# Seven products in place of eight for the left half of the first slice, and for one quarter product of each other slice

## The chip, the cores and the metric

One NeuronCore of a Trainium2 chip runs the whole program. The metric is the device time of one execution in microseconds (us), here the median of three. Every number of the page and the trace comes from one profiled execution; times in the trace count from the start of its span. TensorE multiplies matrices (PE, with PEld for its weight loads), VectorE (DVE) and ScalarE (ACT) do elementwise work, GpSimd (POOL) and SyncE (SP) mostly start transfers. A matmul here has float32 operands, and the trace shows each as two records.

## The reference

Four layers over `x` (8 batches, 2048 nodes, 64 features), each ending in a residual sum and a layernorm. All of them multiply `adj` (2048 x 2048) with the nodes, twice in most layers:

```python
# layer 0: three terms, the node's own weights made from its embedding
As = [I, A, 2 A A - I]
x_g = einsum('knm,bmc->bnkc', stack(As), x)
x = layernorm(x + einsum('bnki,nkio->bno', x_g, einsum('nd,dkio->nkio', emb, weight)) + emb @ bias)
# layer 1: z = relu((A z) w_i), twice.   x = layernorm(x + z)
# layer 2: x = layernorm(x + x w_self + (A x) w_neigh + b)
# layer 3: [x, A x, 2 A A x - x] twice, times weight, + b, then the same
```

The change concerns the first of these products, `A x` of layer 0, and some weights that stand beside it.

## The kernel before

Nodes stand on 128 partitions in 16 tiles, and the 8 batches make 4 pairs of 128 columns: `xy[:, t, slot, pair]`. A product `A x` is 2048 x 2048 by 2048 x 512.

Later products (`product`, from L211) are made of seven quarter products in place of eight, and each quarter product again of seven; the names A11, A12, A22 and S1 to S4 are the seven left operands (quarters of `adj` or sums of quarters). Each needs eight blocks of `adj` or of sums of its blocks, read from DRAM: plain blocks from `in_blocks`, and sums from `comb`, 1 MB a load.

Nothing has made those sums at the start. So the first product runs in the *slice stage*, over four slices `ns` of four row tiles each (tiles `ns`, `ns + 4`, ...). A slice of `adj` is loaded as four chunks of 512 columns (`slice_chunk`, L152, 1 MB each) into a ring of four buffers `a`. While TensorE multiplies a slice, `prepare` (L638) has VectorE form its share of all sums of `adj`, and GpSimd's queue stores them in `comb` (`keep`, L655). `outer` makes S1 to S4 of two half chunks each (tag "T", three buffers; each a pair of sums of 128x1024, so 1 MB), `inner` makes the four inner sums of a quarter (tag "C", four buffers, four sums of 128x512). A chunk's buffer is free when TensorE and all of these sums have read it. The last sum to read chunks 0 and 1 is S3's outer sum.

- *Slice 0* is plain (`plain_slice`, L783): 64 matmuls of 512 columns, in the order of chunks 2, 3, 0, 1 (`AHEAD`), for four pairs into four PSUM banks. Meanwhile VectorE makes the sums, and `sums_of_x` (L749) the four sums T1 to T4 of quarters of x.
- *Slices 1 to 3* (`fast_slice`, L807) use seven quarter products, of 16 matmuls with 256 columns each (`mul`, L825): A12 (`p2`), A22 with T4 (`pd`), A11 (`pa`), S1 with T1, S2 with T2, S4, S3 with T3. The first two read chunks 2 and 3 alone, `pa` chunks 0 and 1. Results are joined in `hT` (`done`, L839), whose copy is stored as `t1T` by SyncE's queue (`keep_t1`, L770) and transposed back into `xy` (`back`, L779, by `to_nodes` L453) between later matmuls.

Loads of chunks, of weights, the `t1T` stores and later `a`, `xT`, `tT` loads all go through SyncE's queue, in an order that the tile scheduler made; GpSimd's queue holds the `comb` stores, `e_sb`, and later its own sums. `wn`, layer 0's weights, is loaded on SyncE's queue at L592 and summed (differences and centring, `sum_wn` L604) in slice 2. It's first used by `feature0` (L954, matmuls at L970) after the first two of the next product's seven quarter products.

Where an instruction is wrapped in `keep_in_program_order`, the scheduler leaves it in the order of the program among those of its engine that are wrapped too. In slice 0 the sums are not wrapped, in slices 1 to 3 they are.

Of the kernel before, what the change touches and what calls it, by code (L numbers as in the profile page):

```python
# [16 lines left out]
P = 128  # L17
# [3 lines left out]


A11, A12, A22, S1, S2, S3, S4 = range(7)

# [77 lines left out]
def kernel(  # L104
# [470 lines left out]


    if True:
        l0 = first.enter_context(tc.tile_pool(name="l0", bufs=1))

        wn = l0.tile([P, 3, D, F], F32, tag="wn", name="wn")  # L580

        def center(w, half=slice(0, P), pin=lambda inst: inst):
            shape = list(w.shape)
            m = small.tile([P, shape[1]], F32, tag="wm", name="wm")[half]
# [3 lines left out]
            ))  # L588

        def load_weights():  # L590
            for k in range(2):
                nc.sync.dma_start(wn[k * F : (k + 1) * F], w_l0.rearrange("n i d o -> i n d o"))  # L592
            nc.gpsimd.memset(wd, 0.0)
            w3 = sums.tile([P, 5, F], F32, tag="t", name="w3", bufs=5)
            for k in range(2):
                half = slice(k * F, (k + 1) * F)
                for i, src in ((W1A, w_l1[0]), (W1B, w_l1[1]), (W2N, w_neigh), (W2S, w_self)):
                    nc.sync.dma_start(wd[half, i, half], src)
                nc.scalar.dma_start(w3[half], w_l3.rearrange("(k i) o -> i k o", i=F))
            nc.sync.dma_start(b2, b_l2.to_broadcast([P, F]))  # L600
            nc.sync.dma_start(b3, b_l3.to_broadcast([P, F]))
            return w3

        def sum_wn():  # L604
            pin = tc.keep_in_program_order
            pin(nc.vector.tensor_tensor(wn[:, 0], wn[:, 0], wn[:, 2], ALU.subtract))
            pin(nc.vector.tensor_scalar(wn[:, 2], wn[:, 2], 2.0, None, ALU.mult))
            center(wn.rearrange("p n d o -> p (n d) o"), pin=pin)

        def sum_weights(w3):  # L610
            pin = tc.keep_in_program_order
# [26 lines left out]
        def prepare(ns, ch, outers):  # L638

            ch = [c.rearrange("p m i n -> p i m n") for c in ch]  # L640

            def add(out, a, b, op=ALU.add):
                inst = nc.vector.tensor_tensor(out, a, b, op)
                if ns:

                    tc.keep_in_program_order(inst)

            def kept(tag, shape, bufs):
                s = sums.tile([P, *shape, GW], F32, tag=tag, name="s" + ("i" if tag == "C" else "o"), bufs=bufs)
                n = "ab"[: len(shape)]  # L650
                return s, s.rearrange(f"p {' '.join(n)} (m n) -> p {' '.join(n)} m n", m=TG)

            def keep(q, s0, src):
                dst = comb[q][s0 : s0 + src.shape[1]].rearrange("s p (n c) -> p s n c", n=TG)
                nc.gpsimd.dma_start(dst[:, :, ns], src)  # L655

            def inner(q, q00, q01, q10, q11):
                flat, s = kept("C", (4,), 4)
                add(s[:, 0], q10, q11)
                add(s[:, 1], s[:, 0], q00, ALU.subtract)  # L660
                add(s[:, 2], q00, q10, ALU.subtract)
                add(s[:, 3], q01, s[:, 1], ALU.subtract)
                keep(q, 4, flat)

            def raw(I, J):
                return [ch[2 * J + b][:, 2 * I + a] for a in range(2) for b in range(2)]

            def outer(a, b, op):

                flat, s = kept("T", (2, 2), 3)  # L670
                for c in range(2):
                    add(s[:, :, c], a(c), b(c), op)
                return flat

            def rq(I, J):
                return lambda c: ch[2 * J + c][:, 2 * I : 2 * I + 2]

            def sq(s):
                return lambda c: s[:, :, c].rearrange("p a (m n) -> p a m n", m=TG)

            def put(q, s):
                flat = s.rearrange("p a b c -> p (a b) c")
                keep(q, 0, flat[:, :2])
                keep(q, 3, flat[:, 3:])
                inner(q, *(flat[:, k].rearrange("p (m n) -> p m n", m=TG) for k in range(4)))


            inner(A12, *raw(0, 1))
            inner(A22, *raw(1, 1))
            outers[S1] = s1 = outer(rq(1, 0), rq(1, 1), ALU.add)  # L690
            outers[S2] = s2 = outer(sq(s1), rq(0, 0), ALU.subtract)
            outers[S4] = s4 = outer(rq(0, 1), sq(s2), ALU.subtract)
            yield
            put(S1, s1)
            yield
            put(S2, s2)
            inner(A11, *raw(0, 0))
            yield
            outers[S3] = s3 = outer(rq(0, 0), rq(1, 0), ALU.subtract)
            yield  # L700
            put(S3, s3)
            put(S4, s4)
            yield

        with tc.tile_pool(name="p_n", bufs=4, space=PSUM) as p_n, tc.tile_pool(
# [30 lines left out]
            def xq(h, c):  # L736

                v = xy[:, h * NT // 2 : (h + 1) * NT // 2, 0, c * 4 * F : (c + 1) * 4 * F]
                return v.rearrange("p (t h) c -> p t h c", h=2)
# [6 lines left out]
                xy[:, 2:NT:TG, 1, :].rearrange("p t (h c) -> p t h c", h=2),  # L746
            ]

            def sums_of_x():  # L749
                sub = ALU.subtract  # L750
                nc.vector.tensor_tensor(T[0], xq(0, 1), xq(0, 0), sub)
                nc.vector.tensor_tensor(T[1], xq(1, 1), T[0], sub)
                nc.vector.tensor_tensor(T[2], xq(1, 1), xq(0, 1), sub)
                nc.vector.tensor_tensor(T[3], xq(1, 0), T[1], sub)

            def join_bias(h, c):
                v = xq(h, c).rearrange("p t h (b f) -> p (t h) b f", f=F)
# [18 lines left out]
            def new_h():  # L776
                return sums.tile([P, GW], F32, tag="t", name="hT", bufs=5)

            def back(ns, p, hT):  # L779
                to_nodes(1, p_tn, slice(ns, NT, TG), p, hT)  # L780
                yield

            def plain_slice(ns, ch):  # L783

                ps = [bank() for p in range(NP)]
                for n, j in enumerate(AHEAD):
                    steps = [(p, m) for p in range(NP) for m in range(TG)]
                    if n == 0:

                        steps = [(p, m) for m in range(TG) for p in range(NP)]  # L790
                    for k, (p, m) in enumerate(steps):
                        mm = nc.tensor.matmul(  # L792
                            ps[p],
                            xcol(0, TG * j + m, p),
                            ch[j][:, m],
                            start=(n == 0 and m == 0),
                            stop=(n == NG - 1 and m == TG - 1),
                            skip_group_check=True,
                        )
                        if n == k == 0:  # L800
                            tc.keep_in_program_order(mm)
                hT = [new_h() for p in range(NP)]
                for p in range(NP):
                    nc.scalar.copy(hT[p], ps[p])
                return hT

            def fast_slice(ns, ch, held):  # L807


                outers = {}  # L810
# [41 lines left out]
                    return u  # L852

                next(parts)
                p2 = mul(bank(), raw(0, 1), x_of(1, 0))
                pd = mul(bank(), raw(1, 1), t_of(4))
                load_chunks(ns + 1, 2, 3)
                for job in held:
                    pump.add(back(*job))
# [1 line left out]
                pa = mul(bank(), raw(0, 0), x_of(0, 0))  # L861
                p1 = sums.tile([P, GW], F32, tag="p1", name="p1")
                nc.scalar.copy(p1, pa)
                q3 = plus("u3", pd, p1)
                done(0, p2, p1)
                if ns == TG - 1:
                    join_bias(0, 1)
# [3 lines left out]
                load_chunks(ns + 1, 0, 1)  # L871
                if ns == 1:
                    sum_weights(w3)
                elif ns == 2:
                    sum_wn()
                else:
                    join_bias(0, 0)
                pb_ = mul(bank(), summed(S2), t_of(2))
                u2 = plus("u2", pb_, p1)
# [13 lines left out]
            for ns in range(TG):  # L893
                ch = [chunks.pop((ns, j)) for j in range(NG)]
                if ns == 0:
                    for n, _ in enumerate(prepare(ns, ch, {})):
                        if n == 1:
                            sums_of_x()
                    hT = plain_slice(ns, ch)
                    w3 = load_weights()  # L900
                    load_chunks(1, *AHEAD)
                    pump.add(biases())
                else:
                    hT = fast_slice(ns, ch, held)
                for p in range(NP):
                    keep_t1(ns, p, hT[p])

                held = []
                for p in range(NP):
                    if ns == TG - 2:  # L910
                        held.append((ns, p, hT[p]))
                    else:
                        pump.add(back(ns, p, hT[p]))
# [20 lines left out]
        if True:  # L934
            p_y = first.enter_context(tc.tile_pool(name="p_y", bufs=3, space=PSUM))
            l0y = first.enter_context(tc.tile_pool(name="l0y", bufs=1))
            e_sb = l0y.tile([P, NT, D], F32, tag="e_sb", name="e_sb")
            nc.gpsimd.dma_start(e_sb, emb)


            order = [
# [51 lines left out]


            RUNS = {S2: NP, S3: NP}
            product(1, then(feature0, 0, gap=4, pool_sq=True), rate=4, runs=RUNS)


    late = p_z = None
# [127 lines left out]
```

## Time and profile before

| | us |
|---|---|
| three runs, median (lowest, highest) | 1670.58 (1670.14, 1670.74) |
| the profiled execution | 1670.91 |
| its span | 1669.1 |
| TensorE busy | 1660.6 |
| VectorE busy | 945.8 |
| slice 0's matmuls | 5.68 to 61.04 |
| slices 1 to 3, up to the first matmul of the next product | 61.04 to 216.15 |

The page gives busy time and instructions of each engine, then the chain of work that ended last, followed back from the last instruction. Groups and pieces read "line engine operation out<-in". A busy TensorE is a pipelined one: the records of one matmul overlap with the next, so what a matmul costs is the distance between starts.

### The profile page before, as it was taken

How to read it: one execution, taken by the hardware profiler on the slowest of the kernel's cores; microseconds unless marked ns; L12 is line 12 of the kernel's file. 1: busy time of each engine (PE TensorE's matmuls, PEld its weight loads, DVE VectorE, ACT ScalarE, POOL GpSimd, SP SyncE). 2: the span in 40 equal slices, each digit the busy share in tenths (PEclk: the TensorE clock that was granted, in tenths of full speed). 3: DMA queues.
4: the chain of work that ended last, by engine and by line, in shares of the span. 5: the costliest groups of instructions: out<-in, count | busy, mean ns of one | idle time of the engine just before them, and what ended most of it. 6: DMA issues, size and time to landing. Idle time of an engine off the chain costs nothing.

```text
span 1669.1 us, 20686 instructions
## 1 busy us (share of the span) xinstructions
PE 1660.6 (99%) x8182; PEld 1046.5 (63%) x8182; DVE 945.8 (57%) x1695; ACT 265.3 (16%) x766; POOL 246.0 (15%) x332
## 2 busy tenths in 40 slices
PE   9999999999999999999999999999999999999998
PEld 4688854444444444444454455589998455579998
DVE  6497884556456456654434365873568344443657
ACT  0100000142143044430010011220001011100001
POOL 1121200254155056650000000000000000000000
PEclk9999999999999999999999999999999999999999
DMA  9898898504603700019877877667888866678884
GB/s 352 331 373 310 302 334 307 189 27 147 227 26 108 271 26 26 26 51 369 286 264 272 308 263 253 229 225 260 297 297 295 306 212 232 229 267 292 316 308 171
DMA packets 82431, 391.52 MB, mean 235 GB/s; under 512 B 8896, under 2 KB 25536, under 8 KB 42784
## 3 DMA queue, kind: packets, MB, share of 16 engines
q1 hardware_dynamic: 69520, 346.78, 58.8%
q0 software_dynamic: 11248, 42.08, 6.6%
q10 hardware_dynamic: 1568, 1.35, 0.3%
q8 instruction: 65, 1.06, 0.3%
q14 instruction: 30, 0.25, 0.0%
HBM read 339.85 MB, written 50.33 MB: 234 GB/s over the span
## 4 chain that ended last, share of the span: by engine, by line
PE 98%; DMA 1%; DVE 0%; ACT 0%; issue 0%; ACTq 0%; DVEq 0%
PE y L970 20%; PE mmb L272 17%; PE mma L272 12%; PE mmc L272 12%; PE mmb L265 9%; PE ps_n L829 8%; PE mma L265 6%; PE mmc L265 6%; PE ps_n L792 3%; PE z L1022 3%; PE z L1051 2%; DMA a<-in_slices 1%; PE pt L1013 1%; DMA xy<-in_x 0%; PE pt_n L457 0%; PE mmd L265 0%
## 5 line engine op out<-in xcount | busy, mean ns | idle before, releaser
L272 PE MATMUL mmb<-a,t 128*128 128x512 f32 x648 | 292.0, 593 | 0.0
L980 DVE SCALAR_TENSOR_TENSOR xy<-y,e_sb,xy 128x128 f32<-128x128 f32 x512 | 179.6, 351 | 141.2 <-PE y L970 125.3
L272 PEld LDWEIGHTS mmb<-a,t 128*128 128x128 f32 x648 | 121.5, 190 | 145.3 <-issue 143.5
L989 POOL TENSOR_TENSOR s<-s 128x512 f32<-128x512 f32 (+2 forms) x192 | 157.1, 818 | 333.4 <-ACT s L984 323.2
L984 ACT ACTIVATE s<-y,e_sb 128x128 f32<-128x128 f32 x512 | 139.0, 382 | 231.8 <-PE y L970 231.8
L223 DVE TENSOR_TENSOR u<-mmb,p 128x512 f32<-128x512 f32 x84 | 57.8, 689 | 181.8 <-PE mmb L272 126.0
L265 PE MATMUL mmb<-t,a 128*128 128x128 f32 x1344 | 156.9, 275 | 0.0
L265 PEld LDWEIGHTS mmb<-t,a 128*128 128x128 f32 x1344 | 153.4, 192 | 0.0
L970 PE MATMUL y<-wn,xT 64*128 64x512 f32 x512 | 131.5, 590 | 0.0
L970 PE MATMUL y<-wn,tT 64*128 64x512 f32 x512 | 131.2, 589 | 0.0
L970 PE MATMUL y<-wn,C 64*128 64x512 f32 x512 | 131.2, 589 | 0.0
L272 PE MATMUL mma<-a,T 128*128 128x512 f32 x256 | 115.5, 594 | 0.0
L272 PE MATMUL mmc<-a,t 128*128 128x512 f32 x216 | 97.3, 592 | 0.0
L287 ACT COPY p<-mma 128x512 f32<-128x512 f32 x42 | 24.6, 586 | 404.4 <-PE mma L272 262.9
L970 PEld LDWEIGHTS y<-wn,xT 64*128 64x128 f32 x512 | 49.3, 187 | 61.2 <-issue 60.7
L970 PEld LDWEIGHTS y<-wn,tT 64*128 64x128 f32 x512 | 49.6, 187 | 60.3 <-issue 60.3
L970 PEld LDWEIGHTS y<-wn,C 64*128 64x128 f32 x512 | 49.6, 187 | 60.3 <-issue 60.3
L272 PE MATMUL mma<-a,xy 128*128 128x512 f32 x192 | 86.7, 593 | 0.0
L272 PEld LDWEIGHTS mma<-a,T 128*128 128x128 f32 x256 | 47.6, 190 | 56.8 <-issue 56.5
L223 DVE TENSOR_TENSOR C<-mmc,C 128x512 f32<-128x512 f32 x48 | 33.2, 692 | 85.9 <-PE mmc L272 75.1
L272 PEld LDWEIGHTS mmc<-a,t 128*128 128x128 f32 x216 | 40.0, 190 | 45.4 <-issue 45.2
L829 PE MATMUL ps_n<-a,xy 128*128 128x256 f32 x288 | 64.7, 380 | 0.1
(140 smaller groups left out, 2047.2 us busy)
## 6 DMA issues: line engine op xcount, KB each, us to landing
a<-comb SPq DMA_DIRECT2D x240, 1024.0 KB, 4.8
a<-in_blocks SPq DMA_DIRECT2D x54, 1024.0 KB, 4.8
comb<-si POOLq DMA_DIRECT2D x28, 1024.0 KB, 10.5
a<-in_slices SPq DMA_DIRECT2D x15, 1024.0 KB, 9.4
comb<-so POOLq DMA_DIRECT2D x16, 512.0 KB, 6.7
comb<-so POOLq DMA_DIRECT2D x16, 256.0 KB, 8.4
t1T<-hT SPq DMA_DIRECT2D x16, 256.0 KB, 4.2
xT<-in_xT SPq DMA_DIRECT2D x16, 256.0 KB, 3.4
```

The lines of the kernel that those rows point to most:

```text
L223: nc.vector.tensor_tensor(out, a, b, op)
L265: nc.tensor.matmul(to, a[:, k, m, :], xb[:, m, :], start=(start and opens and m == 0), stop=(m == TG - 1), skip_group_check=True,)
L272: nc.tensor.matmul(ps, xb[:, m, :], a[:, :, m, :], start=(start and m == 0), stop=(m == TG - 1), skip_group_check=True,)
L287: nc.scalar.copy(p1, pa)
L792: mm = nc.tensor.matmul(ps[p], xcol(0, TG * j + m, p), ch[j][:, m], start=(n == 0 and m == 0), stop=(n == NG - 1 and m == TG - 1), skip_gr ...
L829: nc.tensor.matmul(ps[:, ts(p, GW // 2)], b(k, p), a(k // TG, k % TG), start=(start and p == k == 0), stop=(k == NT // 2 - 1), skip_group_ ...
L970: mm = nc.tensor.matmul(y[:, b, :], terms[n][half, ts(k, P)], wn[half, n, h * DH : (h + 1) * DH, :], start=(n == 0), stop=(n == 2),)
L980: nc.vector.scalar_tensor_tensor(acc, y[:, :, ts(d, F)], e, acc, ALU.mult, ALU.add)
L984: nc.scalar.activation(s[:, d], y[:, :, ts(d, F)], AF.Copy, scale=e)
L989: nc.gpsimd.tensor_tensor(s[:, :n], s[:, :n], s[:, n : 2 * n], ALU.add)
L1022: nc.tensor.matmul(z[:, k, :], aT[:, ts(k, P)], wd[:, w, :], start=(n == 0), stop=(n == len(terms) - 1),)
L1051: nc.tensor.matmul(z[n][:, k], xT[half, ts(k, P)], w[half], start=True, stop=True)
```

## The change

1. *Slice 0, left half.* Chunks 2 and 3 (the right half of `adj`'s columns) are still multiplied plainly, 32 matmuls of 512 columns. Chunks 0 and 1 are the left half: for two halves of rows and two halves of batches there are four quarter products (A11 and a new A21, with two halves of x), and each is now made by `two_level` of seven products with 28 matmuls of 128 columns.
2. *Slices 1 to 3.* A22 with T4 (`pd`) goes through `two_level` too: 28 matmuls of 128 columns in place of 16 of 256.
3. *`two_level`* takes both PSUM buffers of tag "pt" and turns between them. After each group of four matmuls ScalarE copies the bank out, at 128x128; two groups in each sequence add onto the bank that was copied. VectorE then adds up the copies (128x384 and 128x256), and in slice 0 two more sums of 128x256 join the plain half.
4. *More sums on VectorE.* A21's four inner sums (not stored), eight sums of x's blocks (`sums_of_blocks`) and four of T4's blocks (`t4`), 128x512 each. `t1` lies in the second slot of `xy`, `t4` and `part` in pool `xs`.
5. *VectorE's order in slice 0* is now written out, all wrapped. It is: A22, A12, block sums, A11, A21, outer S1, S2, S4; then one `two_level` result, two sums of x, S1's inner sums, the second result, two sums of x, `t4`, the third result, S2's inner sums, the fourth result, outer S3. S3's and S4's inner sums come in slice 1, after its A22. In slices 1 to 3, A22's inner sums come first, ahead of A12's.
6. *`wn`* moves to pool `l0y`, is loaded by GpSimd's queue behind `e_sb`, and is summed after S1 of the next product (`between` of `product`), centred in three parts.

The changed program's order on SyncE puts the four `t1T` stores of slice 0 ahead of the loads of slice 1's chunks 0 and 1, and the loads of its chunks 2 and 3 ahead of those stores.

```diff
-            inner(A12, *raw(0, 1))
-            inner(A22, *raw(1, 1))
+            outers[A22] = inner(A22, *raw(1, 1))
+            yield
+            inner(A12, *raw(0, 1))
+            if ns == 0:
+                sums_of_blocks()
+                outers[A11] = inner(A11, *raw(0, 0))
+                outers[A21] = inner(None, *raw(1, 0))
             outers[S1] = s1 = outer(rq(1, 0), rq(1, 1), ALU.add)
...
-            inner(A11, *raw(0, 0))
+            if ns:
+                inner(A11, *raw(0, 0))
...
+            b1 = [
+                [by_tiles(xy[:, j * TG : (j + 1) * TG, 0, ts(2 * c + p, 2 * F)]) for j in range(2) for p in range(2)]
+                for c in range(2)
+            ]
+            t1 = [[by_tiles(xy[:, c:NT:TG, 1, ts(n, 2 * F)]) for n in range(4)] for c in range(2)]
+            b4 = [T[3][:, 2 * j : 2 * j + 2, :, ts(p, 2 * F)] for j in range(2) for p in range(2)]
...
+            def two_level(raw, sums_, b, t, out):
+                banks = [p_tn.tile([P, TG, P], F32, tag="pt", name="ps_i")[:, 0] for _ in range(2)]
+                pa, pb_ = banks[:: 1 - 2 * (turn[0] % 2)]
+                turn[0] += 1
...
+                def mul(ps, n, x, start, to):
+                    for m in range(TG):
+                        nc.tensor.matmul(
+                            ps, x[:, m // 2, m % 2], s[n](m), start=(start and m == 0),
+                            stop=(m == TG - 1), skip_group_check=True,
+                        )
+                    nc.scalar.copy(to, ps)
+
+                mul(pa, 0, b11, True, part[:, 0])
+                mul(pb_, 5, t2, True, part[:, 1])
+                mul(pa, 1, b21, False, out[:, 0, 0])
+                mul(pb_, 6, t3, False, part[:, 2])
+                mul(pa, 4, t1, True, out[:, 1, 1])
+                mul(pb_, 3, t4, False, out[:, 0, 1])
+                mul(pa, 7, b22, False, out[:, 1, 0])
+                o = out.rearrange("p a b n -> p (a b) n")
+                pin(nc.vector.tensor_tensor(o[:, 1:], o[:, 1:], part[:, 0].unsqueeze(1).to_broadcast([P, 3, P]), ALU.add))
+                pin(nc.vector.tensor_tensor(o[:, 2:], o[:, 2:], part[:, 1:], ALU.add))
...
-                for n, j in enumerate(AHEAD):
+                for n, j in enumerate(AHEAD[:2]):
...
+                for c in range(2):
+                    for I, q in enumerate((A11, A21)):
+                        out = new_out(("u2", "u3")[I])
+                        two_level(lambda i, j: lambda m: ch[j][:, m, 2 * I + i], outers[q], b1[c], t1[c], by_blocks(out))
+                        for p in range(2):
+                            half = ts(I, GW // 2)
+                            keep_in_program_order(nc.vector.tensor_tensor(
+                                hT[2 * c + p][:, half], ps[2 * c + p][:, half], out[:, ts(p, GW // 2)], ALU.add))
+                        yield hT
...
-                pd = mul(bank(), raw(1, 1), t_of(4))
+                for _ in rest:
+                    pass
+                next(parts)
...
+                q3 = new_out("u3")
+                two_level(lambda i, j: lambda m: ch[2 + j][:, m, 2 + i], outers[A22], b4, t4, by_blocks(q3))
...
+                    for _ in range(2):
+                        next(parts)
+                    first4 = plain_slice(ns, ch, outers)
+                    next(first4)
+                    sums_of_x(0)
+                    sums_of_x(1)
+                    next(parts)
+                    next(first4)
+                    sums_of_x(2)
+                    sums_of_x(3)
+                    sums_t(b4, t4)
+                    next(first4)
+                    next(parts)
+                    hT = next(first4)
+                    next(parts)
...
+            wn = l0y.tile([P, 3, D, F], F32, tag="wn", name="wn")
+            for k in range(2):
+                nc.gpsimd.dma_start(wn[k * F : (k + 1) * F], w_l0.rearrange("n i d o -> i n d o"))
...
-            product(1, then(feature0, 0, gap=4, pool_sq=True), rate=4, runs=RUNS)
+            product(1, then(feature0, 0, gap=4, pool_sq=True), sum_wn, rate=4, runs=RUNS)
```

## The prediction

> **What bounds the kernel now.** I read the page's shares first, then the chain of waits, the waits by engine, and the timeline of the stage that the change touches. Fast and plain alike, TensorE is the bound: 99% busy, 98% of the chain, and it waits 1.6 us in the whole run. So every matmul taken out is worth its pitch, and every new wait of TensorE costs its length.
>
> ```profile
> span 1669.1 us, 20686 instructions
> PE 1660.6 (99%) x8182; PEld 1046.5 (63%) x8182; DVE 945.8 (57%) x1695; ACT 265.3 (16%) x766; POOL 246.0 (15%) x332
> PE 98%; DMA 1%; DVE 0%; ACT 0%; issue 0%; ACTq 0%; DVEq 0%
> PE rise L715 <- DVE zero L712: 1.1, 1, 1.1
> ```
>
> Pitches come from unbroken pieces of the chain (start, us, what, records); a matmul is two records. The three lines are widths 512, 256 and 128.
>
> ```profile
> 223.62 3.43 PE mma L272 x8
> 117.71 3.46 PE ps_n L829 x16
> 1102.74 3.57 PE mmb L265 x32
> ```
>
> That is 0.429, 0.216 and 0.1116 us a record: a matmul of 128 columns costs 0.223, 4% over a quarter of 0.858. The next lines are the slice stage by stretches (us of the stretch, then PE, PEld, DVE, ACT, POOL busy, the granted clock, DMA share, GB/s). The DMA engines are as full as TensorE from 7 to 61 us, and VectorE is 89% busy from 82 to 113.
>
> ```profile
> 6.86:33.60 26.74, 26.74 (x63) 11.91 (x64) 16.92 (x17) 1.28 (x1) 2.96 (x4) 1.00 1.02 383
> 33.60:61.00 27.40, 27.40 (x65) 12.13 (x64) 20.48 (x29) 1.75 (x3) 7.60 (x11) 1.00 0.98 381
> 61.00:82.50 21.50, 21.38 (x129) 18.38 (x128) 6.14 (x8) 2.34 (x4) 2.20 (x3) 1.00 0.81 296
> 82.50:113.40 30.90, 30.90 (x146) 27.23 (x144) 27.46 (x60) 1.17 (x2) 8.18 (x13) 1.00 0.99 380
> ```
>
> Last, five single chunk loads from the DMA view (1 MB each, us from issue to landing). They were issued at 61.2, 85.0, 86.1, 96.1 and 97.3 us. The first landed at 80.3, and that is the only place in the slices where TensorE felt a load: 16 records from 78.29 took 4.00 us where the same piece elsewhere takes 3.62.
>
> ```profile
> a<-in_slices SPq DMA_DIRECT2D x1, 1024.0 KB, 19.0
> a<-in_slices SPq DMA_DIRECT2D x1, 1024.0 KB, 6.9
> a<-in_slices SPq DMA_DIRECT2D x1, 1024.0 KB, 9.5
> a<-in_slices SPq DMA_DIRECT2D x1, 1024.0 KB, 9.8
> a<-in_slices SPq DMA_DIRECT2D x1, 1024.0 KB, 12.6
> ```
>
> **Matmuls.** Plain slice: chunks 0 and 1 lose 32 matmuls of 512 columns, 32 x 0.858 = 27.5 us. Four quarter products by 28 matmuls of 128 columns come in: 112 x 0.223 = 25.0. That is -2.5. Each of the three fast slices swaps 16 matmuls of 256 (6.92) for 28 of 128 (6.25): -0.67 each, -2.0. With the 0.4 lost at 78.29, TensorE has 4.9 us to gain. All of it lies on the path.
>
> **Turning two banks.** Each group of four matmuls (0.893 us) ends in a ScalarE copy of its bank, and the next group but one waits for it: about 5 waits a call, 7 calls. The round trip: the last record starts 0.78 after the group and lasts 0.275 (the 128-column record); ScalarE starts 0.04 later (82.13 + 0.60, copy at 82.77); the copy of 128 columns, by 375 ns for 256 and 586 for 512, is 0.27; TensorE follows 0.09 after a copy (215.56 to 215.65). Sum 1.45, against 1.79 to the next use, less 0.1 to 0.2 for the weight load ahead of it. So it fits with 0.1 to 0.2 to spare and costs nothing. The nearest 128-column ScalarE row (L984, 382 ns) uses that up, and a further 0.15 on each of some 40 waits would be 6 us. I take 0.5, as the copy rows lie nearer, and keep 0 and 6.
>
> **VectorE's fixed order, and the chunks that wait for it.** The changed program's order, with pitches of before (0.605 for 128x512, 1.14 for 1024, 2.2 for 2048, 0.1 where a sum needs the one before it): eight sums of A22 and A12 from 16.4 to 21.4; block sums, held by x's third load (24.3), to 28.7; A11 and A21 to 33.8 (chunk 1 lands at 28.2); six outer sums to 40.6; then four times "combine a product" (1.6), with 2 x 2.2, S1 (2.5), 2 x 2.2, t4 (2.5) and S2 (2.5) between: 63.7. Only now come the S3 outer sums, the last readers of chunks 0 and 1: 64.9 and 66.0. These free the ring for the next slice's chunks 0 and 1. TensorE: 33.6 + 25.0 = 58.6; first product and bias matmuls, 6.9 + 2.0, 67.5; a transpose, 67.9; the seven products, 74.2. The A22 sums of slice 1 are ready at 67.4, before 68.8; that is covered, with 1.4 to spare. But at 74.2 TensorE wants chunk 0, issued at 64.9, and at 75.9 chunk 1, issued at 66.0. Before, it wanted chunk 0 17.3 us after its last plain matmul, now 15.6 after, and two loads rather than one are still out by then (before, the third was issued at 47.5).
>
> The second of a pair took 9.5 and 12.6 us, so chunk 1 lands between 75.5 and 78.6 by these. SyncE puts two hT stores (issued 63.4 and 64.0) ahead of it on its queue, each of which took 10 us and more among the stores of sums (15.2 for one issued at 58.4), so I add 1: 76.5 to 79.6. The wait is 0.6 to 3.7; with the 19.0 of the row that also stood behind such stores, 9.1; nothing is the other end, as wn's 1.5 MB no longer stand in this stretch. I take 3.3, near the upper row, because the sums S2, S3 and S4 of slice 0 are stored just then (about 4 MB from 62 to 76 us).
>
> The Trainium skill (DMA: Bandwidth & Descriptors, Anatomy of one DMA) puts a transfer at 2.0 us plus its bytes over 436 GB/s, given for GpSimd's queue. By that, as an estimate, both chunks are there by 73, the wait is nothing, and the change gains 3.9 us. The rows of 6.9 to 19.0 us speak against it, and the sum goes by them.
>
> **wn moves** from SyncE at 16 us to GpSimd's queue behind e_sb (landing near 208 before), and its sums (8.5 us of VectorE) from slice 2 into the first product, after S1. There VectorE idles 2.1 us in every 3.4 (waits before L223 from 254 to 265); I lay 8.5 us among its sums and the bank of A12's first sum is free at 276.4, needed at 278.6: no cost; with that cover gone, up to 2. Its 1.5 MB (3.8 us at 400 GB/s) run beside the hT stores, whose landing holds SyncE's queue (tT waits for t1T), and behind it the product's fifth load: before issued at 220.4, landed in 7.7, needed at 230.3, so 2.2 to spare. Cost 0 to 2.5 (1.6 over that slack, and 0.9 for TensorE coming sooner); I take 0.5, since the spare covers most of it. Nothing behind it on GpSimd's queue is wanted soon: S3's and S4's sums are read some 60 us later.
>
> **Sum**: -4.9 + 0.5 + 3.3 + 0.5 = -0.6. The profiled execution took 1670.9 (span 1669.1 and 1.8 around it), 0.3 above the median 1670.6; so 1670.3 profiled, 1670.0 timed. Of 1670 us, 0.2% is 3.3 us, about what a measurement can tell from no change.
>
> **Rivals.**
> - *The chunks come in time* (wn gone, a short queue): -4.9 + 0.5 + 0.5 = -3.9, 1666.7. For it: 6.9 for the load at 85.0, and few stores between 51 and 62. Against it: every second load took 9.4 or more, and it needs 9.9 with hT stores ahead.
> - *Chunk 1 is as late as at 61.2* (slower): landing at 85, a wait of 9.1, -4.9 + 9.1 + 1 = +5.2, 1675.8. It decides once the wait exceeds 7.2, a landing after 83.1. For it: the same neighbours, hT stores in front and four stores of sums alongside. Against it: up to its issue the DMA engines have some 18 MB to move (8 of inputs, 7 of sums, 2 of chunks, 1 of hT), against 23 before (wn's 1.5, 3 more of sums, 1 more chunk), so less old backlog.
> - *The banks turn too slowly* (slower): 0.2 on each of 40 waits is 8, net +7, 1677. Against it: the worked-out spare.
> - *It doesn't remove what it says*: the changed order does have 28 matmuls of 128 columns for each product, so no chance.
>
> The granted clock is 1.00 in every stretch above, so the sum has no slow clock in it. The Trainium skill (TensorE: Matmul & The Clock Gate, Part 1) says that an idle window of some 3.4 us halves the clock until as long a busy one has passed; no TensorE wait here is that long, and by the page, as an estimate, a single wait over that would add 1.7 us. It speaks against a change that makes TensorE wait for loads; my two waits, about 1.5 and 1.8 us, would stay under it.
>
> **Chances.** Forecast 0.53; in time 0.19; chunk 1 very late 0.16; slow banks 0.12. So faster 0.19, same 0.53, slower 0.28. The forecast alone spans 1667.3 to 1673.5; with enough of the others, 1666.2 to 1676.5.
>
> **What would show it.** Right: 128-column records at 0.112 us; a wait of TensorE for the loads of `a` near 74 and 76 us, 2 to 5 us in all; S3's outer sums near 64 us; product 1's first matmul 1 to 2 us sooner than 216.15. Wrong: many small waits on ScalarE at the seven products, a wait on VectorE there (its order later than my list), a lower clock, or no load wait at all.

## The result and the profile after

The changed kernel takes 1676.13 us (median of 7, 1674.68 to 1677.26); the kernel before took 1670.62 in the same set. The ratio is 1.0032, with a 95% interval of 1.0020 to 1.0043: slower by 5.5 us, where I had forecast no change that can be measured. Its profiled execution is one of the shorter ones, 1674.7 us, 3.8 more than the 1670.9 of the execution shown before.

The page after, first lines and shares of the chain:

```profile
span 1672.9 us, 21268 instructions
PE 1657.7 (99%) x8414; PEld 1061.1 (63%) x8414; DVE 965.5 (58%) x1737; ACT 275.6 (16%) x811; POOL 246.9 (15%) x334
PE 98%; DMA 2%; DVE 0%; issue 0%; SPq 0%; DVEq 0%
```

TensorE is busy 2.9 us less, and the run is longer all the same. The waits of TensorE after (what it waited for, us in total, times, longest) say where:

```profile
PE mmc L273 <- DMA a<-comb: 5.5, 1, 5.5
PE ps_n L902 <- DMA a<-in_slices: 1.7, 1, 1.7
```

The second is the wait for slice 1's chunk that I had forecast. The first is new: 5.5 us, at the next product's fifth load. The chain of waits after shows how it arises (start, us, what):

```profile
211.06 12.76 DMA t1T<-hT
...
224.79 7.64 DMA a<-comb
...
232.56 5.40 PE mmc L273 x8
237.97 3.43 PE mmb L273 x8
```

A t1T store of slice 3, issued at 211.06, lands only 12.76 us later. SyncE's queue stands at the tT load that waits for it, the load of `a` behind that is issued at 224.79, and TensorE, which is ready for it at 227, starts at 232.56. The next eight records then take 5.40 us in place of 3.43. The windows of the same stretch show that this is the clock (the columns as before; the granted clock is the third from the end):

```profile
215.00:225.00 10.00, 10.00 (x25) 4.42 (x24) 9.97 (x9) 1.17 (x2) 0.00 (x0) 1.00 0.97 303
225.00:233.00 8.00, 2.47 (x6) 1.04 (x5) 7.43 (x5) 0.00 (x0) 0.00 (x0) 0.76 0.95 289
233.00:236.00 3.00, 3.00 (x4) 1.04 (x4) 0.00 (x0) 0.00 (x0) 0.00 (x0) 0.50 0.99 418
236.00:240.00 4.00, 4.00 (x11) 1.77 (x10) 2.00 (x2) 0.00 (x0) 0.00 (x0) 0.99 0.85 326
```

The sum closes. The product's first matmul starts at 212.70 in place of 216.15, 3.45 us sooner, and the first matmul of layer 0's weights (`y`) at 316.86 in place of 312.81, 4.05 later. Between them lie 5.5 of wait and 2.0 of slow clock: 7.5, less 3.45, is 4.05. Behind that point little moves: at the end the profiled executions differ by 3.8.

What stood beside those stores is shown by the DMA issues between 196 and 216 us (KB of one, median us to landing).

```profile
comb<-si POOLq DMA_DIRECT2D x2, 1024.0 KB, 15.5
wn<-in_w_l POOLq DMA_DIRECT2D x2, 768.0 KB, 16.9
t1T<-hT SPq DMA_DIRECT2D x4, 256.0 KB, 12.5
```

Before, the four stores of slice 3 took 4.9 us (a DMA line of 210 to 226 us), and SyncE's queue went on soon behind them (below it, start, us, and what SyncE issues):

```profile
t1T<-hT SPq DMA_DIRECT2D x4, 256.0 KB, 4.9
```

```profile
214.51 2.65 SPq L771 DMA_DIRECT2D t1T<-hT  x4
219.23 1.11 SPq L952 DMA_DIRECT2D tT<-t1T  x2
220.43 0.38 SPq L205 DMA_DIRECT2D a<-comb  x1
```

### The profile page after: what moved, and what is told of

Read it like the earlier page. It is cut to its first block, busy times and chain, and to the rows that moved or that the text cites. A ratio compares the mean times of both kernels' runs of the same rounds, so it can differ in the third digit from the quotient of the medians.

```text
span 1672.9 us, 21268 instructions
## 1 busy us (share of the span) xinstructions
PE 1657.7 (99%) x8414; PEld 1061.1 (63%) x8414; DVE 965.5 (58%) x1737; ACT 275.6 (16%) x811; POOL 246.9 (15%) x334
## 4 chain that ended last, share of the span: by engine, by line
PE 98%; DMA 2%; DVE 0%; issue 0%; SPq 0%; DVEq 0%
PE y L1071 20%; PE mmb L273 17%; PE mmc L273 12%; PE mma L273 11%; PE mmb L266 9%; PE ps_n L902 7%; PE mma L266 6%; PE mmc L266 6%; PE z L1123 3%; PE ps_i L816 2%; PE z L1152 2%; PE ps_n L856 2%; PE pt L1114 1%; DMA t1T<-hT 1%; DMA a<-in_slices 1%; DMA a<-comb 0%
## 5 line engine op out<-in xcount | busy, mean ns | idle before, releaser
L1123 PEld LDWEIGHTS z<-wd,C 128*128 128x128 f32 x384 | 50.2, 192 | 21.7 <-issue 20.8
```

Of the source, the lines that this page charges most:

```text
L1123: nc.tensor.matmul(z[:, k, :], aT[:, ts(k, P)], wd[:, w, :], start=(n == 0), stop=(n == len(terms) - 1),)
```

## The experiments

Theory A: the loss is part 6 of the change. wn's two loads now run just ahead of slice 3's stores and make them late, and these hold SyncE's queue. Theory B: TensorE now reaches the product 3.4 us sooner, and the fifth load would be late for that alone, whatever wn does. Beside these stands the small wait for slice 1's chunk, with VectorE's order or the backlog of transfers as its cause. Ratios are against the kernel before on the same chip.

### wn's move alone, in the kernel before

```diff
-            for k in range(2):
-                nc.sync.dma_start(wn[k * F : (k + 1) * F], w_l0.rearrange("n i d o -> i n d o"))
...
-                elif ns == 2:
-                    sum_wn()
...
+            wn = l0y.tile([P, 3, D, F], F32, tag="wn", name="wn")
+            for k in range(2):
+                nc.gpsimd.dma_start(wn[k * F : (k + 1) * F], w_l0.rearrange("n i d o -> i n d o"))
...
-            product(1, then(feature0, 0, gap=4, pool_sq=True), rate=4, runs=RUNS)
+            product(1, then(feature0, 0, gap=4, pool_sq=True), sum_wn, rate=4, runs=RUNS)
```

> The kernel before with only part 6 of the change: wn's loads on GpSimd's queue behind e_sb, its sums after S1 of the next product. Theory A: the t1T stores issued near 214.5 take 11 to 13 us, the fifth load is issued near 227 and lands near 235, 4 to 6 us after 230.3, and eight records behind the wait cost 2 us more: 1676 to 1679. Theory B: TensorE gets there no sooner than before and the stores are done in time: no wait over 1 us, 1670 to 1671.5.

Measured: 1679.43 us, ratio 1.0053 (1.0039 to 1.0066). Its waits, and its chain from the store on:

```profile
PE mmc L272 <- DMA a<-comb: 5.3, 1, 5.3
```

```profile
214.70 12.45 DMA t1T<-hT
...
227.64 7.61 DMA a<-comb
...
235.39 5.71 PE mmc L272 x8
241.10 3.43 PE mmb L272 x8
```

TensorE comes to the product at 215.72, hardly sooner than the 216.15 before, and the same wait is there. The load of `a` is issued at 227.64, 7.2 later than before. This one part costs 8.9 us by the medians, more than the whole change. Theory B falls as the sole cause.

### No load of wn at all

```diff
-            for k in range(2):
-                nc.gpsimd.dma_start(wn[k * F : (k + 1) * F], w_l0.rearrange("n i d o -> i n d o"))
+            nc.gpsimd.memset(wn, 0.0)
```

> The changed kernel with wn set to zero by GpSimd in place of being loaded; it leaves out the true weights of layer 0. Theory A (wn's loads are what makes the stores late): slice 3's t1T stores take 5 to 6 us, the fifth load lands before 227, no wait for it, 1668 to 1669.5, and what is left against the kernel before is the matmuls' 4.5 us less the 1.7 us wait for slice 1's chunk: about 1667.8 by that sum. Theory B (TensorE comes too soon for the queue in any case): a wait of 2 us or more stays, 1671 or more.

Measured: 1667.98 us, ratio 0.9986 (0.9977 to 0.9995); the sum had given 1667.8. The stores are back at the time they took before, and of the two waits only the chunk's is left (a DMA line of the window 210.6 to 214.6, and below it a line of the waits):

```profile
t1T<-hT SPq DMA_DIRECT2D x4, 256.0 KB, 4.9
```

```profile
PE ps_n L902 <- DMA a<-in_slices: 1.3, 1, 1.3
```

So all the rest of the change is worth about 2.8 us, and wn's load takes 8.1 by these medians. TensorE comes to the product at 212.45 here, still sooner than in the changed kernel, and waits for no load there: Theory B falls altogether.

### The first tT loads on another queue

```diff
-                        nc.sync.dma_start(tile_, src[p][:, ts(i, GW)])
+                        queue = nc.gpsimd if k < 2 and src is t1T else nc.sync
+                        queue.dma_start(tile_, src[p][:, ts(i, GW)])
```

> The changed kernel with the first two loads of tT (which wait for the t1T stores) on GpSimd's queue in place of SyncE's; wn stays where the change put it. Theory A, that the queue stands still: the stores still take about 12 us, but the product's fifth load is issued when its buffer is free (near 215 us), lands before 227, and the 7.4 us go: 1667 to 1669. Rival, that the DMA engines have too much to move in this stretch: the load is issued early and still lands after 229, a wait of 2 us or more stays, 1671 to 1676.

Measured: 1669.46 us, ratio 0.9993 (0.9985 to 1.0002), 6.7 us less than the changed kernel. Waits and chain:

```profile
PE mmc L273 <- DMA a<-comb: 1.4, 1, 1.4
PE ps_n L902 <- DMA a<-in_slices: 0.9, 1, 0.9
```

```profile
215.64 3.12 SPq L768
...
218.85 9.07 DMA a<-comb
...
228.06 3.67 PE mmc L273 x8
```

The stores still take 12.8 us, but nothing of TensorE's stands behind them: the held queue is the path of the loss. My rival is right for a remainder: the load was issued at 218.85, not near 215, since SyncE itself spent 5.1 us in issuing the fourth store (213.66 to 218.76; the chain holds the last 3.12), and the load then took 9.07 us. The changed kernel's fourth store took SyncE 5.1 us too; before, and in the run without wn's load, it took 0.6. A wait of 1.4 stays, and no slow clock follows it.

### wn later, on SyncE's queue

```diff
+            def load_wn():
+                for k in range(2):
+                    tc.keep_in_program_order(
+                        nc.sync.dma_start(wn[k * F : (k + 1) * F], w_l0.rearrange("n i d o -> i n d o"))
+                    )
...
+        if ahead is not None:
+            ahead()
         inner(S1, t1, *fresh(v))
```

> The changed kernel with the two loads of wn (768 KB each) put on SyncE's queue behind the seventh load of the next product, in place of GpSimd's queue behind e_sb; everything else on both queues keeps its order. Theory A (wn's loads run beside slice 3's four t1T stores, these land 8 us later, SyncE's queue stands before tT, and the product's fifth load comes late): the stores take about 5 us again in place of 12.5, the fifth load lands before TensorE wants it near 227 us, the wait of 5.5 us and the slow matmuls behind it (5.40 us for eight records in place of 3.43) go. That is 7.4 us less: 1667.3 by the profiled execution of the changed kernel, some 1668 by its median. Theory B (TensorE reaches the product 3 to 4 us sooner than before, and loads behind such stores are late whatever wn does): the wait stays at 3 us or more, 1673 to 1677.

Measured: 1674.7 us (1673.26 to 1679.01), ratio 1.0026 (1.0015 to 1.0038). The profiled execution is the longest of them, 1679.0; its chunk wait is 2.3 us and is followed by a slow clock too, and in slice 1's seven products TensorE waits 1.0 us for VectorE's inner sums, as in no other run. The wait near 227 is gone, and the stores take 5.4 us. Neither theory saw what came in its place (waits, then chain):

```profile
PE mma L273 <- DMA a<-comb: 4.4, 1, 4.4
```

```profile
231.29 14.53 DMA a<-comb
...
245.96 6.29 PE mma L273 x8
```

A load of 1 MB behind wn's two took 14.53 us, about three times its usual 4.7 there. The window in which wn's loads run shows why (the last two columns are the share of the DMA engines and GB/s):

```profile
228.50:231.50 3.00, 3.00 (x8) 1.33 (x7) 2.67 (x3) 0.00 (x0) 0.00 (x0) 1.00 1.02 429
234.00:243.50 9.50, 7.56 (x18) 3.04 (x16) 9.50 (x9) 0.00 (x0) 0.00 (x0) 1.00 1.02 236
```

The DMA engines are full in both, but move 429 GB/s with the `a` loads and 236 with wn's. In the trace, wn's 384 packets of 4 KB take 318 ns each here (mean), where those of 4 KB on GpSimd's queue in the kernel before took 159 (median). Together they fill the 16 DMA engines for 7.6 us (384 x 318 ns / 16), twice what I had laid out.

### As many bytes for all partitions

wn's loads fill 64 partitions each. Here each fills 128, from rows of `adj`.

```diff
-                nc.gpsimd.dma_start(wn[k * F : (k + 1) * F], w_l0.rearrange("n i d o -> i n d o"))
+                row = slices[0, k].rearrange("p m n c -> p (m n c)")
+                nc.gpsimd.dma_start(wn.rearrange("p n d o -> p (n d o)")[:, ts(k, 3 * DH * F)], row[:, : 3 * DH * F])
```

> The changed kernel with wn's two loads of 768 KB each made of as many bytes of adj, but each for all 128 partitions (6 KB a partition) in place of 64 (12 KB a partition); both come ahead of the last two stores of sums on GpSimd's queue, where the changed kernel has one ahead and one behind. It leaves out the true weights of layer 0. In the run with wn on SyncE's queue the packets of wn's loads, 4 KB each, took 318 ns where other 4 KB packets take 159, and the core moved 200 to 246 GB/s at a full DMA share. Theory P (a load that fills 64 partitions alone gets half the rate, so wn costs 1.5 MB at some 205 GB/s, 7.3 us, and not the 3.8 us that I laid out): with 128 partitions it is 3.7 us, slice 3's t1T stores land near 220.3 in place of 223.8, the product's fifth load near 229, the wait shrinks from 5.5 to about 2 us, and the slow matmuls behind it go: about 1671 by the median. Theory Q (its bytes cost the same however they are laid): the wait stays at 5 us and the time at 1675 to 1677.

Measured: 1671.05 us, ratio 1.0002 (0.9993 to 1.0010); Theory P had said about 1671. The stores take 10.2 us, the wait is 2.4, and the packets of 6 KB take 234 ns (median), 26 bytes a ns against 13 for wn's. So of the 8.1 us that wn's load costs, 5.1 went with this edit. The Trainium skill (SBUF — State Buffer, Door 1: The DMA port swizzle) has a reason for a factor of two: partitions 0 to 63 lie on 8 of the memory's 16 DMA ports, the others on the other 8. The two rates agree with it; the ports themselves are in no trace. The size of the packets, their source and the order of wn's second load on its queue differ too, and none was tried alone, so for the 5.1 the half of the partitions is the likely cause and not one that is shown. One part of my expectation was wrong, that the slow clock would go:

```profile
226.50:229.50 3.00, 0.58 (x3) 0.06 (x1) 2.67 (x3) 0.00 (x0) 0.00 (x0) 1.00 1.01 429
229.50:232.90 3.40, 3.40 (x4) 1.33 (x5) 3.27 (x3) 0.00 (x0) 0.00 (x0) 0.51 1.00 424
```

### S3's outer sums sooner in slice 0

```diff
             put(S1, s1)
             yield
+            if ns == 0:
+                s3 = outer(rq(0, 0), rq(1, 0), ALU.subtract)
+                yield
             put(S2, s2)
...
-            outers[S3] = s3 = outer(rq(0, 0), rq(1, 0), ALU.subtract)
-            yield
+            if ns:
+                outers[S3] = s3 = outer(rq(0, 0), rq(1, 0), ALU.subtract)
+                yield
```

> The changed kernel with slice 0's S3 outer sums put ahead of S2's inner sums, before the fourth seven-product result, so that the last reads of chunks 0 and 1 by VectorE come some 5 us sooner; SyncE then loads slice 1's chunks 0 and 1 behind two of the four t1T stores. If VectorE's order makes these loads late, they are issued near 60 us, land before 74, and the wait of 1.7 us near 75.5 goes: 1.7 us less, 1673.0 profiled and about 1674.4 by the median. If it is the backlog of transfers, the loads land no sooner than 76 to 77 us and nothing changes: 1676.

Measured: 1673.87 us, ratio 1.0020 (1.0011 to 1.0028), 2.3 less than the changed kernel. Its two chunk loads are issued at 61.16 and 62.30 and land at 66.8 and 71.5. TensorE goes from the seven products into them without a gap, and only the wait of 5.6 us at the product is left:

```profile
68.61 6.30 PE ps_i L820 x56
74.91 3.46 PE ps_n L906 x16
```

So this wait was VectorE's order (with the place of the stores on SyncE's queue, which moved along), not a backlog.

### All three taken away

S3 sooner, the first tT loads on GpSimd's queue, and wn in six loads of 256 KB, each behind one of the next product's ninth to fourteenth loads:

```diff
+            for n in (0, 2, 1):
+                for k in range(2):
+                    pieces.append((wn[k * F : (k + 1) * F, n], w_l0.rearrange("n i d o -> i n d o")[:, n]))
...
+        if ring2 is None and loads <= 2 * (RING + 3):
+            tc.keep_in_program_order(fetched)
+            if loads > RING + 4:
+                tc.keep_in_program_order(nc.sync.dma_start(*pieces.pop(0)))
```

> The kernel with S3's outer sums sooner (as in the run on VectorE's order), the first two loads of tT on GpSimd's queue, and wn in six loads of 256 KB on SyncE's queue, one behind each of the next product's ninth to fourteenth load. If the loss is wn's loads beside the stores, the held queue and VectorE's order, each can be taken away: 1676.1 less 7.4 less 2.3, about 1666.4, faster than the kernel before by 4 us, which is what the matmuls alone are worth (4.5). Rival: wn's slow loads delay the loads around them wherever they stand; a wait of 2 us or more near 240 to 260, 1668.5 to 1674.

Measured: 1666.68 us (1665.13 to 1668.62), ratio 0.9976 (0.9966 to 0.9986): faster than the kernel before by 4.1 us, and than the changed one by 9.5. TensorE waits for no load any more; its whole list is

```profile
PE rise L720 <- DVE zero L717: 1.1, 1, 1.1
PE pt_n L463 <- ACT xy L464: 0.3, 1, 0.3
```

The slow pieces make the loads around them take up to 9.7 us, which the ring of four hides.

### The changed kernel again

> The changed kernel itself once more, since its profiled execution (1674.7 us) is near the lowest of its seven (1674.7 to 1677.3, median 1676.1). If the spread comes from the waits for loads and from how long the clock stays low behind them, this execution differs from the first by the wait near 227 us (5.5 us), the eight records behind it (5.40 us) and the wait near 75.5 us (1.7 us), and in nothing else: by up to 2.5 us in all. If it comes from elsewhere, these three stay as they are while the time differs by over 1 us.

> The same, for a further execution: expected as for the look before it.

Measured: 1675.8 and 1675.4 us, with waits of 5.9 and 5.8 us at the product and 2.3 and 2.0 for the chunk; the eight records took 5.40 and 5.43. The waits of the first are 1.0 us above those of the execution shown, its time 1.1; of the second 0.6, its time 0.7. So nearly all of that spread is in the two waits; the longest executions were not traced.

## Why the prediction was wrong, point by point

- **Matmuls, -4.9: right.** The 224 records of the four quarter products took 25.01 us, as summed; the 56 of a fast slice 6.25 and 6.30. With no wait left, the product starts 5.15 us sooner than before (211.00 against 216.15). Chain of the changed kernel:

```profile
33.02 25.01 PE ps_i L816 x224
58.03 3.46 PE ps_n L902 x16
...
119.41 6.30 PE ps_i L816 x56
```

- **Turning two banks, +0.5: it costs nothing.** 25.01 / 224 is 0.1117 a record, the unbroken pitch, and no wait of the seven products on ScalarE stands in the list. The copy rows were the nearer ones; that rival is gone.
- **VectorE's order and the chunks, +3.3: right mechanism, too large by 1.3.** I had the chunk loads issued at 64.9 and 66.0 and chunk 1 landing at 76.5 to 79.6, wanted at 75.9. They were issued at 65.30 and 66.66, took 7.62 and 10.53 us, and chunk 1 landed at 77.19, wanted at 75.5. The wait was 1.7, and 0.3 was lost in the records behind it. I had leaned to the upper row because of stores of sums alongside; the second of a pair took what such a second took before.
- **wn moves, +0.5 within 0 to 2.5: this step failed.** The chain of events was the one I wrote down (the stores late, tT holding SyncE's queue, the fifth load behind it), but the term measured 7.5 us, three times its upper bound. Two numbers were mis-sized. The first is the price of wn's load. I had 3.8 us, 1.5 MB at 400 GB/s; beside it the stores took 7.6 longer (12.5 against 4.9). With part 6 alone the load of `a` was issued 7.2 later, and TensorE came 0.4 sooner: 7.2 + 0.4, less the 2.2 to spare, is 5.4, and 5.3 was measured. In the changed kernel the stores were issued 3.45 sooner, so the load's issue came only 4.4 later (224.79 against 220.43), and TensorE came to it 3.3 sooner (227.0 against 230.3): 4.4 + 3.3, less 2.2, is 5.5. So TensorE's coming sooner, for which the sum held 0.9, changed the wait little; the stores move with it. The second number is the slow clock: 2.0 came on top, and the sum held none, because both the waits in it were short. Nor had the 0.5 a reason of its own: the spare that should cover most of the cost had been taken off already in the 1.6 that make the bound of 2.5 with the 0.9. The price came from the rate of the full DMA engines; what was wanted was how long this one load, in its own shape, keeps them in its new place. The trace of before could not show that: there wn's packets ran among stores of sums in slice 0, and took 159 ns (median) as others of 4 KB did.
- **wn's sums on VectorE, 0: right.** No wait of TensorE on VectorE appears in the first product.
- **The rivals.** None had its place where the loss was. Both slower ones were about the slices; the term that decided the sign had been put away as a bound of 2.5. Taking 7.5 for the 0.5, 2.0 for the 3.3, nothing for the banks and 5.15 for the matmuls gives +4.35 in place of -0.6, against a measured +3.8 in the profiled execution; where the last 0.5 lies was not traced.
- **The signs named.** The 128-column records, the chunk wait near 76 us (one, not two) and S3's outer sums (63.4 to 65.8) came as written. The product began 3.45 us sooner, not 1 to 2; that alone said that the slices had gone better than the sum, and that the loss was behind them.

## What to carry to other kernels

A transfer that is moved is not only a time at which its data is needed: ask which stores and loads it will run beside, what waits for those to land, and which queue that wait holds. Where a queue waits for a store, put the loads that TensorE needs next on another queue or ahead of it. Price a load by its own shape and its neighbours: one to 64 partitions held the DMA engines here for up to twice as long as its bytes suggest, and it cost nothing that could be seen in small pieces where the loads around it had some microseconds to spare. A sum that makes TensorE wait should also ask whether the clock will fall behind the wait.

## What the runs showed of the hardware that I had not expected

- *A load to half of the partitions can halve the rate of the whole core while it runs*: with wn later, 236 GB/s at a full DMA share against 429, packets of 318 ns against 159. What it runs beside matters: among stores of sums in slice 0 before, wn's packets took 159 ns (median). In the changed kernel all packets of 4 KB on GpSimd's queue from 190 to 230 us filled the 16 engines for 18.9 us, without wn's load for 13.0; that leaves some 5.7 us for wn (an estimate), against 3.8 at 159 ns a packet. The Trainium skill (DMA: Bandwidth & Descriptors, Rules for kernel authors) says that two transfers to disjoint halves are better made as one of 128 partitions, which is what the 1671.05 against 1676.13 agree with.
- *Whether the clock fell was not decided by the length of the wait alone.* A wait of 2.4 was followed by a granted clock of 0.51 over the next 3.4 us, and eight records took 5.37 us in place of 3.43; one of 2.3 (for the chunk, in the run with wn later) by 0.64 over 3.1 us, and eight records of 3.04 in place of 1.73. Waits of 1.4, 1.7 and 2.0, and one of 2.3 in the changed kernel's second execution, were followed by no low clock.
- *One rule fits every case in these traces.* The granted clock is 1.00 or 0.50 in them, and from its first rise on it changes only at whole multiples of 3.413 us. So the time can be cut into windows of that length. Each window ahead of a fall had TensorE busy for 16 to 36% of it; those with a wait in which it was busy for 53% or more had none behind them; no case lies between. The two waits of 2.3 us, both 2.29, differ in this. With wn later the whole wait lay in one window, 77.16 to 80.57 us (TensorE busy 1.12 us of it), and the clock was 0.50 until 83.99. In the changed kernel's second execution a bound at 76.69 split it (busy 2.37 us in one window, 2.17 in the next), and the clock stayed at 1.00. The Trainium skill (TensorE: Matmul & The Clock Gate, Part 1) gives an idle window of about 3.4 us and says that the windows run freely; length and free running agree, but a window did not have to be idle throughout.
- *The price follows from the windows and not from the wait*: 1.9 to 2.9 us of slow matmuls (the prediction had named 1.7 by the skill's page) behind waits of 2.4, 4.4, 5.3, 5.5, 5.6, 5.8 and 5.9 us. The clock stayed low for one window or for two, and what counts is how much of them TensorE worked: 3.4 us behind the wait of 2.4 (1.9 lost), 5.3 behind the one of 4.4 (2.9 lost), 3.5 behind the one of 5.5 (2.0 lost).
